# A gated state scan behind an attention layer: its plan of steps rearranged, with two gate buffers and the transposed product kept in its source's tile

## The chip, the cores and the metric

The kernel runs on one core of one Trainium2 chip. The metric is the device time in microseconds (us) of one execution. The chip's engines run side by side, each through its own queue in order: PE (TensorE: matrix products, PEld being its weight loads), DVE (VectorE), ACT (ScalarE), POOL (GpSimd) and SP, which only issues DMA transfers here. They wait for each other through semaphores.

## What is computed

Two layers are added to a residual stream `x` of 8 batches, 1024 time steps and 512 channels in float32. The first is a modulated attention; the change doesn't touch it. The second, cut to what matters:

```python
xr, gate = jnp.split(x @ W_in.T, 2, axis=-1)          # 1024 + 1024 channels
xc = jax.nn.silu(conv4(xr + t_emb) + b_conv)          # causal, 4 taps, by channel
xn = (xc - mu) / jnp.sqrt(var + 1e-05) * ln_g + ln_b
Bm, Cm, dt = jnp.split(xn @ W_xproj.T, 3, axis=-1)    # 16 states
dt = jnp.tanh(dt @ W_dt.T + b_dt) * 0.01
Ad = 1.0 + dt * A                                     # A = -tanh(A_log)
Bd = Bm * jnp.minimum(norm(xn), 1.0)
h = jnp.clip(h * ad[:, :, None] + bd[:, :, None] * xt[:, None, :], -10.0, 10.0)   # over time
yt = jnp.einsum('bd,bdh->bh', ct, h)
y = ys + D * xn
return y * jax.nn.silu(gate) @ W_out.T
```

The recurrence in `h` must run through the 1024 time steps one after the other. Its state is 8 batches x 16 states = 128 rows by 1024 channels, one tile of the chip's 128 partitions.

## The kernel before

`network` runs `modulated_attention` and then `gated_scan`. Inside `gated_scan` the order is written by hand: `at(n, f, ...)` (line 492) puts a piece of work into the list of step n, and the last loop (line 818) walks through the steps, issuing first `step(n)`, the recurrence, and then the pieces of step n in the order in which they were put there. Each engine's queue has exactly this order, so a piece that waits holds up all that comes after it on the same engine.

A chunk is 32 time steps (`TC`) of all 8 batches; there are 32 chunks. A chunk has two halves (i = 0 and 1) of 16 steps, each a tile of 128 rows (16 times x 8 batches). `n0` is the first step of a chunk and `p0 = n0 - 32`, so the pieces put at `p0 + ...` prepare a chunk while the one before runs, and those at `n0 + ...` or later finish it. Steps are counted within a chunk, 0 to 31, below. The pieces are:

- Preparation: `load_x1` (512 KB of the stream, by DMA), eight input products with the convolution (`conv_mm` on PE, `conv_in` on ACT, `conv_taps` on DVE, `conv_out` on ACT), then the normalization by halves: `flip_mm` (PE transposes, "x flips"), `stats` and `center` (DVE), `deviation`, `scale` (which also stores the tile `xt` as `xd` in HBM), `squares` (ACT), and `skip` (DVE, `xt` times D). `p_mm`, `p_out`, `p_flip`, `lengths`, `params`, `params_mm` and `params_out` make the 48 parameters of each time step; `spread` sends them over the partitions with eight small DMAs into `bca`; `decay` turns them into factors (tanh on ACT at line 630, then seven DVE instructions), and `weights` fills the weights `yw` of the state products.
- Recurrence: `fetch` brings four time steps at once, spread over the 16 states, with eight DMAs of 256 KB (three buffers `xb`); `weigh` scales one step's row on ACT two steps ahead; `step` is one DVE instruction that writes `h` (line 755; a pool `hp` of six buffers); `products`, the state products on PE, read four `h` tiles at once at steps 0, 4, 8, ... and add up `y_ps`.
- Output by halves: `order` (ACT) copies the stream in the half's row order into `x1t`; `gate_mm` (PE, two halves of 512 columns) and `gate` (ACT, silu) make the gate; `gate_y` (DVE) adds `y_ps` to `xt` and multiplies by the gate; `out_flip` (PE) and `out_copy` (ACT) transpose the product into `gT`; `out_mm` (PE, two halves, the first with an identity product that adds the stream) makes `o_ps`; `out_store` copies and stores it.

The tiles in question: `gate` and `gT` have one buffer each, `xt` four, `x1t` two, `y_ps` two (two PSUM banks each), and all other PE outputs share the four remaining banks (tag "mm"). Every DMA is issued by SP, in the plan's order.

The plan around the change is in lines 762 to 811; the gate's and the output's pieces are placed by two lines:

```python
g0 = n0 + (4, 20)[i]          # order at g0, gate products at g0 + 3 and g0 + 5
e0 = n0 + TT * i + TT         # gate_y at e0 + 2, flips at e0 + 4, 5, output products at e0 + 7, 9
```

Of the kernel before, what the change touches and what calls it, by code (L numbers as in the profile page):

```python
# [8 lines left out]
F32 = mybir.dt.float32  # L9
# [6 lines left out]
P = 128  # L16
# [5 lines left out]
DI = 1024  # L22
KI = DI // P
NS = 16
TC = 32
TT = 16
# [338 lines left out]
def gated_scan(ctx, tc, const, x1_d, S, w_in, w_conv, cols, ln_g, ln_b, w_x, w_xd, w_dt, b_dt, a_log,  # L365
# [10 lines left out]
    nc = tc.nc  # L376
    NCH = S // TC
    CW = B * TC
    NT = TC // TT
# [3 lines left out]
    one = ctx.enter_context(tc.tile_pool(name="s1", bufs=1))  # L383
    two = ctx.enter_context(tc.tile_pool(name="s2", bufs=2))
    hp = ctx.enter_context(tc.tile_pool(name="hp", bufs=6))
    xcp = ctx.enter_context(tc.tile_pool(name="xcp", bufs=2))
    xtp = ctx.enter_context(tc.tile_pool(name="xtp", bufs=4))
# [30 lines left out]
    na = load(a_log, "na", [P, 1])  # L418
    wx_sb = wp.tile([P, KI, NX], F32, name="wx")
    nc.sync.dma_start(out=wx_sb[:, :, 0 : 2 * NS], in_=w_x.rearrange("(k p) o -> p k o", p=P))  # L420
    wxd = one.tile([NS, DI], F32, tag="gT", name="wxd")
    nc.sync.dma_start(out=wxd, in_=w_xd)
    wdt = load(w_dt, "wdt", [NS, NS])
    my_sb = load(mask_y, "mask_y", [P, B])
# [67 lines left out]
    def at(n, f, *args):  # L492
        plan.setdefault(n, []).append(lambda: f(*args))
# [173 lines left out]

    def gate(st, i, half):
        if half == 0:
            st["gate", i] = one.tile([P, DI], F32, name="gate")  # L670
        nc.scalar.activation(
            st["gate", i][:, half * 512 : (half + 1) * 512], st.pop(("g", i, half)), AF.Silu
        )

    def gate_y(st, i):
        xt, g = st.pop(("xt", i)), st["gate", i]
        nc.vector.tensor_add(xt, st.pop(("y", i)), xt)
        nc.vector.tensor_mul(g, xt, g)  # L678

    def out_flip(st, i, half):  # L680
        ps = st["gt", i, half] = ps_m.tile([P, 4, P], F32, tag="mm", name="gt_ps")
# [3 lines left out]

    def out_copy(st, i, half):
        if half == 0:
            st["gT", i] = one.tile([P, KI, P], F32, tag="gT", name="gT")
        nc.scalar.copy(st["gT", i][:, 4 * half : 4 * half + 4, :], st.pop(("gt", i, half)))  # L689

    def out_mm(st, i, half):
# [70 lines left out]
    for c in range(NCH):  # L762
        st, n0 = sts[c], c * TC
        p0 = n0 - TC
        if c > 0:
            at(p0 - 11, load_x1, st, c)
        at(p0 - 9, begin, st)
        for k in range(KI):
            at(p0 - 8 + 2 * k, conv_mm, st, k)
            at(p0 - 7 + 2 * k, conv_in, st, k)  # L770
            at(p0 - 5 + 2 * k, conv_taps, st, k)
            at(p0 - 4 + 2 * k, conv_out, st, k)
        for i in range(NT):
            f0 = p0 + 11 + 3 * i
            at(f0, flip_mm, st, i, 0)
            at(f0, flip_mm, st, i, 1)
            at(f0 + 1, stats, st, i, 0)
            at(f0 + 1, stats, st, i, 1)
            at(f0 + 1, center, st, i)
            at(f0 + 2, deviation, st, i)  # L780
            at(f0 + 3, scale, st, i)
            at(f0 + 4, squares, st, i)
            at(f0 + 7 + i, skip, st, i)
        at(p0 + 12, p_mm, st)
        at(p0 + 13, p_out, st)
        at(p0 + 15, p_flip, st)
        at(p0 + 19, lengths, st)
        for i in range(NT):
            at(p0 + 20 + i, params, st, i)
            at(p0 + 21 + i, params_mm, st, i)  # L790
            at(p0 + 22 + i, params_out, st, i)
        at(p0 + 23, spread, st)
        at(p0 + 26, decay, st)
        at(p0 + 28, weights, st, 0)
        at(n0 + 4, weights, st, 1)
        for i in range(NT):
            g0 = n0 + (4, 20)[i]
            at(g0, order, st, i)
            for half in range(2):
                at(g0 + 3 + 2 * half, gate_mm, st, i, half)  # L800
                at(g0 + 5 + 2 * half, gate, st, i, half)
            e0 = n0 + TT * i + TT
            at(e0 + 2, gate_y, st, i)
            for half in range(2):
                at(e0 + 4 + half, out_flip, st, i, half)
                at(e0 + 5 + half, out_copy, st, i, half)
                at(e0 + 7 + 2 * half, out_mm, st, i, half)
            at(e0 + 11, out_store, st, c, i)
    for g in range(S // 4):
        at(4 * g - 9, fetch, g)  # L810
        at(4 * g + 4, products, g)
# [13 lines left out]
@with_exitstack  # L825
def network(ctx: ExitStack, tc: tile.TileContext, S, ins, out):
    nc = tc.nc
    const = ctx.enter_context(tc.tile_pool(name="const", bufs=1))
    dram = ctx.enter_context(tc.tile_pool(name="dram", bufs=1, space=DRAM))
    x1_d = dram.tile([S // TC, H, B, TC], F32, name="x1_d")  # L830
    xu_d = dram.tile([2, H, S], F32, name="xu_d")
    ident = const.tile([P, P], F32, name="ident")
    nc.sync.dma_start(out=ident, in_=ins["ident"])
    sT = const.tile([P, 2 * KH, B], F32, name="sT")
    nc.sync.dma_start(out=sT, in_=ins["condT"].rearrange("(k p) b -> p k b", p=P))
    with tc.manual_schedule():
        modulated_attention(
            tc, const, x1_d, xu_d, S, ins["xT"], {n: ins[f"w{n}T"] for n in "qkvwu"}, ident, sT
        )
        gated_scan(  # L840
            tc, const, x1_d, S, ins["w_in"], ins["w_conv"],
            {n: ins[f"{n}_c"] for n in ("b_conv", "ln_g", "ln_b")}, ins["ln_g"], ins["ln_b"],
            ins["w_x"], ins["w_xd"], ins["w_dt"], ins["b_dt"], ins["a_log"], ins["d_skip"],
            ins["w_out"], ident, ins["cond"], ins["pick"], ins["mask_y"], out,
        )
# [62 lines left out]
```

## Time and profile before

| | |
|---|---|
| median of 3 runs | 6852.26 us (6847.03 to 6880.9) |
| the profiled execution | 6840.93 us, span 6838.9 us |
| mean granted TensorE clock | 0.947 |
| PE, DVE, ACT busy in 5000 to 6000 us | 849, 761, 648 us |
| DMA engines busy there, and what they moved | 0.78, 202 GB/s |
| the recurrence instruction (line 755) | 1024 x 1342 ns, 587.5 us idle before it |
| the scaling (line 731) | 1024 x 1140 ns |
| gate products (line 663), output products (line 701) | 460.5 and 468.0 us in all |

A span is the time from the first to the last instruction. A chunk of the second layer takes some 95 us, and the second layer some 3100 of the 6839 us. "Busy" is the time in which an engine executes; "idle before" a group of instructions is what its engine stood still just ahead of them, with the instruction that released it. In the timeline a row gives the start in us from the start of the span, the length, the engine, the line, the operation, the tiles (written <- read) and, in brackets, the idle time and the releaser.

### The profile page before, as it was taken

The numbers are of one execution on the slowest core, as the hardware profiler recorded it, in microseconds if no ns is written. First come the engines' busy times: TensorE is split into PE (matmuls) and PEld (weight loads), VectorE is DVE, ScalarE is ACT, GpSimd is POOL, SyncE is SP. The second block draws the span as 40 slices with busy tenths as digits, with TensorE's granted clock in tenths as the row PEclk, the third lists the DMA queues.
The fourth block names the chain that finished last, engine by engine and source line by source line (L and its number), as shares of the span: only waits on it lengthen the run. The fifth ranks groups of instructions, "written<-read, shape, count | busy, mean of one in ns | idle before, by whom it ended". The sixth has DMA issues, their size and how long they took to land.

```text
span 6838.9 us, 113125 instructions
## 1 busy us (share of the span) xinstructions
PE 6072.8 (89%) x42960; PEld 3291.8 (48%) x42960; DVE 4499.3 (66%) x6851; ACT 3919.7 (57%) x6713; POOL 1333.6 (20%) x1220
## 2 busy tenths in 40 slices
PE   7889989899899898998997788888888888888887
PEld 4555545555555455555554444444434444444443
DVE  2656656656566566565664677777777777777776
ACT  3555545545555455555553566666666666666665
POOL 2343333423433334234332000000000000000000
PEclk9999999999999999999999898999889998899898
DMA  2011111111111111111112777778777787777776
GB/s 67 18 32 50 46 43 41 30 55 44 33 49 46 43 44 29 57 43 37 44 34 75 192 202 202 199 197 208 202 196 204 199 209 200 196 203 196 202 205 174
DMA packets 493518, 777.47 MB, mean 114 GB/s; under 512 B 197008, under 2 KB 295448, under 8 KB 492976
## 3 DMA queue, kind: packets, MB, share of 16 engines
q1 hardware_dynamic: 492976, 770.22, 43.3%
q8 instruction: 342, 5.60, 0.3%
q14 instruction: 200, 1.64, 0.1%
HBM read 659.40 MB, written 83.89 MB: 109 GB/s over the span
## 4 chain that ended last, share of the span: by engine, by line
PE 64%; DVE 17%; DMA 7%; ACT 4%; issue 4%; SPq 2%; POOL 1%; DVEq 0%; ACTq 0%; POOLq 0%
PE mm_ps L107 17%; PE t_ps L245 12%; PE s_ps L235 7%; PE av L252 7%; DVE h L755 7%; PE o_ps L701 5%; PE g_ps L663 4%; DMA xb<-xd 4%; PE y_ps L742 3%; PE in_ps L508 3%; DVE nmax L327 2%; PE p_ps L539 2%; SPq L724 1%; ACT xb L731 1%; DVE gate L678 1%
## 5 line engine op out<-in xcount | busy, mean ns | idle before, releaser
L755 DVE CUSTOM_DVE_ANT_0 h<-h,xb,lim 128x1024 f32<-128x1024 f32 x1024 | 1374.1, 1342 | 587.5 <-ACT xb L731 335.2
L327 DVE TENSOR_REDUCE nmax<-s_ps 128x1 f32<-128x1024 f32 x1024 | 1205.0, 1218 | 767.6 <-PE s_ps L238 763.7
L356 POOL TENSOR_SCALAR pr<-pr,rinv 128x1024 f32<-128x1024 f32 x1024 | 1148.2, 1122 | 2279.5 <-PE t_ps L245 1515.8
L245 PEld LDWEIGHTS t_ps<-ident,pr 128*128 128x128 f32 x8192 | 904.7, 141 | 868.1 <-issue 609.0
L245 PE MATMUL t_ps<-ident,pr 128*128 128x128 f32 x8192 | 1156.7, 280 | 170.3 <-DVE pT L338 124.8
L336 ACT ACTIVATE pr<-s_ps,nmax 128x1024 f32<-128x1024 f32 x1024 | 1141.5, 1115 | 83.9 <-DVE nmax L327 60.3
L731 ACT ACTIVATE xb<-xb,ws 128x1024 f32<-128x1024 f32 x1024 | 1154.0, 1140 | 30.8 <-DMA xb<-xd 30.8
L333 ACT COPY pT<-t_ps 128x512 f32<-128x512 f32 x512 | 300.1, 586 | 1313.6 <-PE t_ps L245 1313.6
L742 PE MATMUL y_ps<-h,yw 128*32 128x512 f32 x4096 | 647.1, 720 | 8.0 <-DVE h L755 8.0
L346 DVE COPY pT<-t_ps 128x512 f32<-128x512 f32 x512 | 353.2, 690 | 399.9 <-PE t_ps L245 397.7
L235 PE MATMUL s_ps<-kT,qT 32*128 32x512 f32 x2048 | 579.7, 640 | 0.0
L238 PE MATMUL s_ps<-k,q 32*128 32x512 f32 x2048 | 577.1, 640 | 0.0
L252 PE MATMUL av<-pT,vt 128*32 128x128 f32 x16384 | 559.2, 278 | 0.4 <-DVE aT L319 0.4
L508 PE MATMUL in_ps<-x,win 128*128 128x256 f32 x2048 | 543.2, 412 | 3.6 <-DMA x<-x_d 2.8
L508 PEld LDWEIGHTS in_ps<-x,win 128*128 128x128 f32 x2048 | 401.2, 205 | 162.8 <-issue 59.2
L701 PE MATMUL o_ps<-wout,gT 128*128 128x512 f32 x1024 | 468.0, 600 | 0.5 <-ACT gT L689 0.5
L252 PEld LDWEIGHTS av<-pT,vt 128*32 128x32 f32 x16384 | 420.1, 110 | 88.0 <-issue 86.6
L663 PE MATMUL g_ps<-win,x1t 128*128 128x512 f32 x1024 | 460.5, 592 | 0.4 <-ACT x1t L658 0.4
L527 DVE SCALAR_TENSOR_TENSOR xc<-xr,cw,xc 128x256 f32<-128x256 f32 x768 | 370.7, 483 | 26.7 <-ACT xc L520 8.4
L338 DVE COPY pT<-t_ps 128x512 f32<-128x512 f32 x512 | 348.4, 680 | 2.6 <-PE t_ps L245 2.6
L347 ACT COPY pT<-t_ps 128x512 f32<-128x512 f32 x512 | 297.4, 581 | 82.2 <-PE t_ps L245 82.2
L684 PE MATMUL gt_ps<-ident,gate 128*128 128x128 f32 x512 | 108.8, 350 | 243.7 <-DVE gate L678 243.7
(128 smaller groups left out, 6381.5 us busy)
## 6 DMA issues: line engine op xcount, KB each, us to landing
xb<-xd SPq DMA_DIRECT2D x2048, 256.0 KB
xd<-xt SPq DMA_DIRECT2D x64, 512.0 KB
xh<-in_xT SPq DMA_DIRECT2D x16, 1024.0 KB
q<-qT SPq DMA_DIRECT2D x128, 128.0 KB
xr<-in_xT SPq DMA_DIRECT2D x64, 256.0 KB
xu_d<-xr SPq DMA_DIRECT2D x64, 256.0 KB
xr<-xu_d SPq DMA_DIRECT2D x64, 256.0 KB
x_d<-xr SPq DMA_DIRECT2D x64, 256.0 KB
```

What stands on the lines that cost most here:

```text
L107: nc.tensor.matmul(ps, w, x, start=(k == 0), stop=(k == KH - 1))
L235: nc.tensor.matmul(s_ps[i][:, 0:HW], st["q"][r, qc], st["k"][r, 0:HW], start=True, stop=True)
L245: nc.tensor.transpose(ps[:, j], pr[:, c0 : c0 + P], ident)
L252: nc.tensor.matmul(av[r], vt[:, kt, r], pT[:, i, kt], start=(kt == 0), stop=(kt == KT - 1), skip_group_check=True,)
L327: nc.vector.tensor_reduce(nmax[i], s_ps[i], AX.X, ALU.max, negate=True)
L336: nc.scalar.activation(fresh[i], s_ps[i], AF.Exp, bias=nmax[i], accum_out=rsum[i])
L356: nc.gpsimd.tensor_scalar(fresh[i], fresh[i], rinv[i], 1.0, ALU.mult, ALU.mult)
L508: nc.tensor.matmul(ps, win_sb[:, kk, k * P : (k + 1) * P], st["x1"][:, kk].rearrange("p b t -> p (b t)"), start=(kk == 0), stop=False,)
L701: nc.tensor.matmul(ps, st["gT", i][:, k, :], wout_sb[:, k, :], start=False, stop=(k == KI - 1), skip_group_check=True,)
L731: nc.scalar.mul(xbs[n], xbs[n], sts[c]["ws"][:, t : t + 1])
L742: nc.tensor.matmul(st["y", i][32 * r : 32 * r + 32, hf * 512 : (hf + 1) * 512], yws[i][:, 4 * q + r, :], hs[4 * g + r][:, hf * 512 : (hf + ...
L755: nc.vector._custom_dve(dve_ops.TENSOR_ADD_SAT, out=h, in0=last["h"], in1=xbs.pop(n), s0=lim[:, 0, t : t + 1], s1=lim[:, 1, t : t + 1],)
```

## The change

The pieces of the plan are moved, and some tiles change. The first gate product of half 0 goes from step 7 to 1 and the second from 9 to 5; those of half 1 from 23 and 25 to 22 and 23. `gate_y` is split into `add_y` and `gate_y`, a step or two apart; half 0 is at 23 and 24 (before 18), half 1 at 8 and 10 of the next chunk (before 2). The output products of half 0 go from 23 and 25 to 27 and 29, those of half 1 from 7 and 9 to 13 and 15. The `gate` tile gets two buffers, since it now lives longer; the transposed product has no tile `gT` of its own any more and is written into the tile `xt` of its half, and `wxd`, which shared that buffer at the start, moves to the pool of `xt`. In the preparation the second half's normalization stands four steps after the first one's (before three), `skip` at 19 and 25 (before 18 and 22), and the parameters' pieces from `p_mm` to `weights` one step later, `spread` among them. On PE the number of products is the same.

```diff
--- before.py
+++ after.py
@@ -418,7 +418,7 @@
     na = load(a_log, "na", [P, 1])
     wx_sb = wp.tile([P, KI, NX], F32, name="wx")
     nc.sync.dma_start(out=wx_sb[:, :, 0 : 2 * NS], in_=w_x.rearrange("(k p) o -> p k o", p=P))
-    wxd = one.tile([NS, DI], F32, tag="gT", name="wxd")
+    wxd = xtp.tile([NS, DI], F32, tag="xt", name="wxd")
     nc.sync.dma_start(out=wxd, in_=w_xd)
     wdt = load(w_dt, "wdt", [NS, NS])
     my_sb = load(mask_y, "mask_y", [P, B])
@@ -667,15 +667,17 @@
 
     def gate(st, i, half):
         if half == 0:
-            st["gate", i] = one.tile([P, DI], F32, name="gate")
+            st["gate", i] = two.tile([P, DI], F32, name="gate")
         nc.scalar.activation(
             st["gate", i][:, half * 512 : (half + 1) * 512], st.pop(("g", i, half)), AF.Silu
         )
 
+    def add_y(st, i):
+        nc.vector.tensor_add(st["xt", i], st.pop(("y", i)), st["xt", i])
+
     def gate_y(st, i):
-        xt, g = st.pop(("xt", i)), st["gate", i]
-        nc.vector.tensor_add(xt, st.pop(("y", i)), xt)
-        nc.vector.tensor_mul(g, xt, g)
+        g = st["gate", i]
+        nc.vector.tensor_mul(g, st["xt", i], g)
 
     def out_flip(st, i, half):
         ps = st["gt", i, half] = ps_m.tile([P, 4, P], F32, tag="mm", name="gt_ps")
@@ -685,7 +687,7 @@
 
     def out_copy(st, i, half):
         if half == 0:
-            st["gT", i] = one.tile([P, KI, P], F32, tag="gT", name="gT")
+            st["gT", i] = st.pop(("xt", i)).rearrange("p (k t) -> p k t", k=KI)
         nc.scalar.copy(st["gT", i][:, 4 * half : 4 * half + 4, :], st.pop(("gt", i, half)))
 
     def out_mm(st, i, half):
@@ -771,7 +773,7 @@
             at(p0 - 5 + 2 * k, conv_taps, st, k)
             at(p0 - 4 + 2 * k, conv_out, st, k)
         for i in range(NT):
-            f0 = p0 + 11 + 3 * i
+            f0 = p0 + 11 + 4 * i
             at(f0, flip_mm, st, i, 0)
             at(f0, flip_mm, st, i, 1)
             at(f0 + 1, stats, st, i, 0)
@@ -780,32 +782,33 @@
             at(f0 + 2, deviation, st, i)
             at(f0 + 3, scale, st, i)
             at(f0 + 4, squares, st, i)
-            at(f0 + 7 + i, skip, st, i)
-        at(p0 + 12, p_mm, st)
-        at(p0 + 13, p_out, st)
-        at(p0 + 15, p_flip, st)
-        at(p0 + 19, lengths, st)
+            at(p0 + (19, 25)[i], skip, st, i)
+        at(p0 + 13, p_mm, st)
+        at(p0 + 14, p_out, st)
+        at(p0 + 16, p_flip, st)
+        at(p0 + 20, lengths, st)
         for i in range(NT):
-            at(p0 + 20 + i, params, st, i)
-            at(p0 + 21 + i, params_mm, st, i)
-            at(p0 + 22 + i, params_out, st, i)
-        at(p0 + 23, spread, st)
-        at(p0 + 26, decay, st)
-        at(p0 + 28, weights, st, 0)
+            at(p0 + 21 + i, params, st, i)
+            at(p0 + 22 + i, params_mm, st, i)
+            at(p0 + 23 + i, params_out, st, i)
+        at(p0 + 24, spread, st)
+        at(p0 + 27, decay, st)
+        at(p0 + 29, weights, st, 0)
         at(n0 + 4, weights, st, 1)
-        for i in range(NT):
-            g0 = n0 + (4, 20)[i]
-            at(g0, order, st, i)
+
+        for i, (xo, gm, gs, ey) in enumerate(
+            ((-2, (1, 5), (3, 7), (23, 24, 25, 27)), (17, (22, 23), (24, 25), (40, 42, 43, 45)))
+        ):
+            at(n0 + xo, order, st, i)
+            at(n0 + ey[0], add_y, st, i)
+            at(n0 + ey[1], gate_y, st, i)
             for half in range(2):
-                at(g0 + 3 + 2 * half, gate_mm, st, i, half)
-                at(g0 + 5 + 2 * half, gate, st, i, half)
-            e0 = n0 + TT * i + TT
-            at(e0 + 2, gate_y, st, i)
-            for half in range(2):
-                at(e0 + 4 + half, out_flip, st, i, half)
-                at(e0 + 5 + half, out_copy, st, i, half)
-                at(e0 + 7 + 2 * half, out_mm, st, i, half)
-            at(e0 + 11, out_store, st, c, i)
+                at(n0 + gm[half], gate_mm, st, i, half)
+                at(n0 + gs[half], gate, st, i, half)
+                at(n0 + ey[2] + half, out_flip, st, i, half)
+                at(n0 + ey[2] + 1 + half, out_copy, st, i, half)
+                at(n0 + ey[3] + 2 * half, out_mm, st, i, half)
+            at(n0 + ey[3] + 4, out_store, st, c, i)
     for g in range(S // 4):
         at(4 * g - 9, fetch, g)
         at(4 * g + 4, products, g)
```

## The prediction

> **What bounds the kernel now.** I read the page first. The work splits near 3750 us, where POOL falls silent and the DMA share rises from 1 to 7 tenths. The diff touches only the second part.
>
> ```profile
> PE 6072.8 (89%) x42960; PEld 3291.8 (48%) x42960; DVE 4499.3 (66%) x6851; ACT 3919.7 (57%) x6713; POOL 1333.6 (20%) x1220
> ...
> POOL 2343333423433334234332000000000000000000
> ...
> DMA  2011111111111111111112777778777787777776
> ...
> PE 64%; DVE 17%; DMA 7%; ACT 4%; issue 4%; SPq 2%; POOL 1%; DVEq 0%; ACTq 0%; POOLq 0%
> ```
>
> No engine is saturated in that part. By the windows view, 5000 to 6000 us has PE busy 849 us, VectorE 761, ScalarE 648, DMA engines 0.78. So the limit must alternate. The next view is the timeline of VectorE over one chunk (start us, length, engine, line, tiles, then idle time and releaser). The lines are the recurrence steps h(2), h(6), h(10), ... of a chunk; I number them from h(18), the only one followed by the add, the gate product and a skip product (L677, L678, L595; 5199.96).
>
> ```profile
> 5152.00 1.34 DVE L755 CUSTOM_DVE_ANT_0 h<-h,xb,lim 128x1024 f32<-128x1024 f32 x1
> ...
> 5163.35 1.34 DVE L755 CUSTOM_DVE_ANT_0 h<-h,xb,lim 128x1024 f32<-128x1024 f32 x1 [0.53 <-PE y_ps L742]
> ...
> 5176.10 1.34 DVE L755 CUSTOM_DVE_ANT_0 h<-h,xb,lim 128x1024 f32<-128x1024 f32 x1 [4.15 <-ACT xs L534]
> ...
> 5189.38 1.35 DVE L755 CUSTOM_DVE_ANT_0 h<-h,xb,lim 128x1024 f32<-128x1024 f32 x1 [1.35 <-PE y_ps L742]
> ...
> 5199.96 1.34 DVE L755 CUSTOM_DVE_ANT_0 h<-h,xb,lim 128x1024 f32<-128x1024 f32 x1
> ...
> 5210.68 1.34 DVE L755 CUSTOM_DVE_ANT_0 h<-h,xb,lim 128x1024 f32<-128x1024 f32 x1
> ...
> 5224.01 1.34 DVE L755 CUSTOM_DVE_ANT_0 h<-h,xb,lim 128x1024 f32<-128x1024 f32 x1 [6.52 <-ACT xb L731]
> ...
> 5237.96 1.34 DVE L755 CUSTOM_DVE_ANT_0 h<-h,xb,lim 128x1024 f32<-128x1024 f32 x1
> ...
> 5246.48 1.34 DVE L755 CUSTOM_DVE_ANT_0 h<-h,xb,lim 128x1024 f32<-128x1024 f32 x1
> ```
>
> The reader should take differences: 11.35, 12.75, 13.28, 10.58, 10.72, 13.33, 13.95 and (5237.96 to 5246.48) 8.52 us; in all 94.48 us a chunk. Brackets hold the waits: 0.53, 4.15, 1.35, 6.52. Step h(n) overwrites the h buffer of step n-6 (six buffers), which the state product of its group reads (L742, planned at steps 0, 4, 8, ...). So at every h(4g+2) VectorE waits until PE has finished everything queued ahead of product 4g. The chunk is eight such meetings, and each stretch lasts as long as the slower of the two engines.
>
> The PE timeline of the same chunk shows how much that is, and the other cost:
>
> ```profile
> 5155.88 1.09 PE L684 MATMUL gt_ps<-ident,gate 128*128 128x128 f32 x4 [3.14 <-DVE gate L678]
> 5156.76 3.62 PE L508 MATMUL in_ps<-x,win 128*128 128x256 f32 x8
> ...
> 5163.65 1.89 PE L508 MATMUL in_ps<-x,win 128*128 128x256 f32 x8
> ...
> 5170.53 3.60 PE L663 MATMUL g_ps<-win,x1t 128*128 128x512 f32 x8
> ...
> 5219.46 1.97 PE L508 MATMUL in_ps<-x,win 128*128 128x256 f32 x8 [0.29 <-DMA x<-x_d]
> ...
> 5223.83 3.70 PE L701 MATMUL o_ps<-wout,gT 128*128 128x512 f32 x8
> ```
>
> A warm input product is 2.5 us (5163.65, with its 0.69 us end piece), a gate product 3.43 to 3.6, a second output product 3.54 to 3.7. After the idle 3.14 us before 5155.88 the same input product takes 3.62 instead of 1.89. The granted clock of 5155.8 to 5161 is 0.50, of 5161 to 5180 it is 1.00.
>
> Last the SP queue of the same chunk:
>
> ```profile
> 5206.11 5.01 SPq L724 DMA_DIRECT2D xb<-xd  x8
> 5211.23 0.57 SPq L401 DMA_DIRECT2D x<-x_d  x1
> 5214.37 5.53 SPq L626 DMA_DIRECT2D bca<-few  x8
> 5220.01 5.49 SPq L724 DMA_DIRECT2D xb<-xd  x8
> ```
>
> The x1 load goes out behind eight fetches (5.0 us after h(19)); the chain of waits gives its transfer 8.09 us, to 5219.34, and PE takes it up at 5219.46 after idling 0.29.
>
> **What the Trainium skill says.** (1) "TensorE: Matmul & The Clock Gate", "HAM oscillation": PE idle for more than about 3.4 us falls back to half clock. The trace agrees: 3.14 us idle was followed by clock 0.50 and doubled durations. (2) Same page, "Architectural detail": ScalarE and VectorE are strict FIFO. Agrees: the scaling of xb stood at 5222.87 behind a gate activation and a conversion that waited 1.29 and 2.34 us for PE. (3) "DMA: Bandwidth & Descriptors", "Queues, rings and completion order": each DMA engine takes descriptors in ring order, so a small load waits behind large ones. Agrees: 8.09 us for x1's 512 KB, behind 2 MB of fetches.
>
> **The change, by stretch.** No arithmetic is removed or added: the sum, product, flips and copies are the same, only split or renamed. I price units from start to next start in those timelines. VectorE: h 1.26 (1.51 if another h follows), taps 1.43, add 1.20, gate product 1.14 (2.39 together), skip 1.14, statistics and centring 2.90, small rs 0.27, scale 1.19, nr 0.60, parameters 0.82, decay 1.49, yw 0.41. PE: input product 2.50, state product 1.85, gate product 3.43, output product 4.43 (first half, with its identity part) and 3.54, gate flip 0.50, x flips 0.97, p 3.58, pt 0.34, xp 0.49. Each stretch (us) runs from h(4g-2) to h(4g+2); PE's load is what it must do after one state product up to and with the next.
>
> | to | VectorE before | PE before | measured | VectorE after | PE after |
> |---|---|---|---|---|---|
> | h(2) | 8.40 | 6.85 | 8.52 | 8.40 | 10.39 |
> | h(6) | 10.70 | 7.35 | 11.35 | 8.56 | 10.28 |
> | h(10) | 8.40 | 12.71 | 12.75 | 9.35 | 7.78 |
> | h(14) | 8.71 | 13.37 | 13.28 | 9.60 | 3.82 |
> | h(18) | 10.59 | 3.16 | 10.58 | 9.65 | 14.71 |
> | h(22) | 10.81 | 2.35 | 10.72 | 8.79 | 1.85 |
> | h(26) | 6.93 | 13.69 | 13.33 | 9.34 | 12.19 |
> | h(30) | 9.80 | 13.82 | 13.95 | 10.30 | 12.28 |
>
> Example: to h(26) before, PE has flip 0.50, xp 2 x 0.49, output 4.43, gate 3.43, input 2.50, state 1.85 = 13.69. After, the output half and the flip are gone from it and the second gate half has come in: 2 x 3.43 + 0.98 + 2.50 + 1.85 = 12.19. The larger of the two, summed: before 94.09 (measured 94.48), after 10.39 + 10.28 + 9.35 + 9.60 + 14.71 + 8.79 + 12.19 + 12.28 = 87.59. That is 6.5 us a chunk less, because the four stretches where gate and output halves stood together (12.7 to 13.8) are spread over five, and one of them (to h(18)) becomes the worst at 14.71.
>
> What gives some of it back, with bounds:
> - To h(18): first output half, p and second output half stand ahead of the second x flips. The statistics of step 16 wait for those flips and are followed by 2.90 us of VectorE, so the stall comes late in the stretch. Output half 1 may start when state product 12 is done, about 1.9 us after h(12). Then flips end 4.43 + 3.58 + 3.54 + 0.97 = 12.5 later, 14.4; with 2.90 and h(17) 1.53, h(18) is 18.8 after h(12). The table has h(12) to h(18) at 5.69 (4.16 + 1.53) + 14.71 = 20.4, so nothing is lost: 0. Against that, gate flips (step 11) wait for the product of step 10: PE is done 7.78 after h(6), that product ends at 9.35 + 1.26 + 1.14 = 11.75, so PE idles 4.0, longer than the 3.14 that preceded clock 0.50. Flips, state product 12 and the start of the output half then run slow: 0 to 3 us, I take 1.2.
> - To h(26): less PE work ahead uncovers the x1 load. h(19) ends 3.7 after h(18); + 5.0 issue + 8.1 transfer + 2.50 + 1.85 = 21.2, against 8.79 + 12.19 = 20.98. I take 0.3; if the load's wait (some 3 us of idle PE) cools the clock, up to 2.5 more. Nothing the change does moves that load; its old release, the reordering copy one step before it, now stands four steps before and never was last.
> - ScalarE, FIFO: h(n+1) of an odd step waits for a scaling queued behind the conversion that needs PE's input product; where PE leads the stretch (to h(2), h(6)) that is 0 to 1, I take 0.3.
> - The spread of bca is one step later, so on SP it is behind the fetch of step 23 (5.0 us), not ahead of it. Behind its tanh on ScalarE stand a conversion and the scaling of h(29); behind decay on VectorE stand taps and h(28). x1 lands at 3.7 + 5.0 + 8.1 = 16.8 after h(18); the last fetch and then the last spread follow. With 6.51 us for a fetch (chain of waits) the last spread is issued near 24, and lands at most 4.0 later (before, 5219.90 to the tanh at 5223.91 without a wait). Tanh near 26.5 (25 to 28), then 0.3 + decay 1.49 + taps 1.43 + h 1.51 + h, yw, taps 3.10 = 7.8: h(30) at 34.3 against 20.98 + 12.28 = 33.3. Some of that overlaps the x1 term; I take 0.5, bounds 0 and 3.
> - Second gate buffer, transposed product in xt (its gate product has been read before the copy, by order), wxd: cost 0, hidden since the tiles' previous users are ten steps or more back; the one tight one, centring at step 16 into xt whose last reader is the output half of step 15, follows x flips that stand behind that half on PE anyway. At the start and end of the part: once, a few us either way, 0.
>
> Sum: -6.5 + 1.2 + 0.3 + 0.3 + 0.5 = -4.2 us a chunk. Of 32 chunks 31 are whole periods: -130 us. Against the profiled execution (span 6838.9, time 6840.93) that is 6711; the median of the runs is 11.3 above it, so 6852 - 130 = 6722.
>
> **Rivals.**
> A, forecast: 6722, its own range 6680 to 6770 (terms at -5.5 to -2.7).
> B, the give-back is hidden: the bare -6.5 x 31 = -200, 6650. For it: before, the bare sum missed by only 0.4 although that chunk had three cooled PE stretches (clock 0.50, 0.66 and 0.67 in 5155.8 to 5161, 5195 to 5200 and 5203 to 5212). Against: before, those cooled stretches fell where VectorE led, and the x1 load was just covered.
> C, the cold clock and x1 take most: terms of 4.5 up to 3 + 2.8 + 0.5 = 6.3, so -2 to 0 a chunk, 6790 to 6852. For it: idle 3.14 us sufficed to halve the clock. Against: PE's queue after the idle is mostly what has 5 us to spare (9.60 against 3.82).
> D, slower: bca. If the eight pieces, queued behind 2 MB, land one after another and not within 4.0, tanh comes past 30 instead of 26.5. The gain to h(30) is 38.0 measured (5199.96 to 5237.96) minus 33.3; the other five stretches give only 56.48 - 54.33 = 2.2, less 1.5 of the terms. So no gain is left from h(30) at 38.0 + 0.7 (tanh at 30.9); with tanh at 33 it is +2.1 us a chunk, +65, about 6917. For it: SP and DMA share 0.9 in 5222 to 5250. Against: pieces of 6 KB landed in 4.0 or less behind x1.
>
> **How the numbers follow.** A 0.50, B 0.17, C 0.19, D 0.14. Time: that of A, 6722. The range leaves out the better part of D's and a corner of B's: 6630 (B, 20 lower) to 6870 (C and D's beginning). A measurement here can tell about 0.5%, 34 us. Faster: A, B and half of C, 0.77; the rest of C 0.09; D 0.14.
>
> **What would show it.** Right: stretches near the last columns; output and gate halves no longer adjacent on PE; a stretch to h(18) of 14 to 16 us with the statistics (L557) waiting for x flips; PE waiting for the x1 DMA some 3 us a chunk; chunk period 89 to 91. Wrong: a wait of ScalarE at L630 for bca over 4 us (D); granted clock low from step 11 to 14 and the stretch over 18 us (C); a period under 88 (B).

## The result and the profile after

The changed kernel takes 6810.5 us (median of 6 runs, 6805.32 to 6819.54) against 6846.35 before (6842.43 to 6880.9, 6 runs): a ratio of 0.9931 (0.9911 to 0.9952), 36 us or 0.7% faster. The forecast was 130 us faster. So the direction is right, the size is less than a third of it, and the time lies where rival C put it (6790 to 6852).

The page of the profiled execution (span 6817.7 us); for the groups the columns are count, busy time, mean ns, idle time before and its releaser:

```profile
PE 6117.6 (90%) x42960; PEld 3331.8 (49%) x42960; DVE 4491.4 (66%) x6851; ACT 3915.2 (57%) x6713; POOL 1329.4 (19%) x1220
...
PEclk9999999999999999999999799999999999999999
DMA  2011111111111111111112787878878778888787
...
L757 DVE CUSTOM_DVE_ANT_0 h<-h,xb,lim 128x1024 f32<-128x1024 f32 x1024 | 1374.2, 1342 | 582.5 <-ACT xb L733 305.0
...
L508 PE MATMUL in_ps<-x,win 128*128 128x256 f32 x2048 | 548.2, 415 | 116.7 <-DMA x<-x_d 116.7
```

The clock line has got better (nearly all 9; before, several slices of the second part were 8), but the input product (L508) now stands 116.7 us behind the DMA of x1, where before 2.8 of its 3.6 idle us were put to that. Next the timeline of VectorE for one chunk, the same eight meetings h(2), h(6), ..., h(30), h(2) as before the change:

```profile
5152.01 1.34 DVE L757 CUSTOM_DVE_ANT_0 h<-h,xb,lim 128x1024 f32<-128x1024 f32 x1
...
5162.39 1.34 DVE L757 CUSTOM_DVE_ANT_0 h<-h,xb,lim 128x1024 f32<-128x1024 f32 x1
...
5172.78 1.34 DVE L757 CUSTOM_DVE_ANT_0 h<-h,xb,lim 128x1024 f32<-128x1024 f32 x1
...
5182.41 1.34 DVE L757 CUSTOM_DVE_ANT_0 h<-h,xb,lim 128x1024 f32<-128x1024 f32 x1
...
5198.57 1.34 DVE L757 CUSTOM_DVE_ANT_0 h<-h,xb,lim 128x1024 f32<-128x1024 f32 x1
...
5207.06 1.34 DVE L757 CUSTOM_DVE_ANT_0 h<-h,xb,lim 128x1024 f32<-128x1024 f32 x1
...
5221.76 1.34 DVE L757 CUSTOM_DVE_ANT_0 h<-h,xb,lim 128x1024 f32<-128x1024 f32 x1 [5.44 <-ACT xb L733]
...
5233.97 1.34 DVE L757 CUSTOM_DVE_ANT_0 h<-h,xb,lim 128x1024 f32<-128x1024 f32 x1
...
5244.38 1.34 DVE L757 CUSTOM_DVE_ANT_0 h<-h,xb,lim 128x1024 f32<-128x1024 f32 x1
```

The differences are 10.38, 10.39, 9.63, 16.16, 8.49, 14.70, 12.21 and 10.41 us. The bracket at h(26) is to be read with care: the scaling of that step had ended 7.8 us earlier (the one that ends at 5221.76 is that of step 27), and what ended 0.11 us before h(26), in this chunk and in the mean of 28, is PE's state product of step 24.

The table puts the means over 28 chunks (third to thirtieth), worked out from the starts of the recurrence instruction in the timelines, beside the larger of the two loads of the prediction:

| stretch to | before | forecast load | after | after minus load |
|---|---|---|---|---|
| h(6) | 11.90 | 10.28 | 10.38 | 0.10 |
| h(10) | 12.46 | 9.35 | 10.38 | 1.03 |
| h(14) | 13.28 | 9.60 | 9.63 | 0.03 |
| h(18) | 10.58 | 14.71 | 15.91 | 1.20 |
| h(22) | 10.74 | 8.79 | 8.49 | -0.30 |
| h(26) | 13.00 | 12.19 | 16.17 | 3.98 |
| h(30) | 13.95 | 12.28 | 12.45 | 0.17 |
| h(2) | 8.54 | 10.39 | 10.36 | -0.03 |
| chunk | 94.45 | 87.59 | 93.77 | 6.18 |

Five stretches are within 0.3 us of their loads. One has nearly all of the loss: h(22) to h(26), where the first input product of the next chunk needs x1. SP's queue and PE's timeline in that place (the rows before 5200 belong to the stretches before it and are used further down):

```profile
5202.39 5.04 SPq L726 DMA_DIRECT2D xb<-xd  x8
5207.54 0.52 SPq L401 DMA_DIRECT2D x<-x_d  x1
5210.42 5.78 SPq L726 DMA_DIRECT2D xb<-xd  x8
5216.78 8.06 SPq L626 DMA_DIRECT2D bca<-few  x8
```

```profile
5175.40 1.09 PE L686 MATMUL gt_ps<-ident,gate 128*128 128x128 f32 x4 [5.41 <-DVE gate L680]
5176.28 1.91 PE L552 MATMUL x_ps<-ident,xs 128*128 128x128 f32 x8
...
5193.51 1.04 PE L552 MATMUL x_ps<-ident,xs 128*128 128x128 f32 x8
...
5215.79 3.38 PE L508 MATMUL in_ps<-x,win 128*128 128x256 f32 x8 [3.74 <-DMA x<-x_d]
5219.10 0.69 PE L512 MATMUL in_ps<-few 8*128 8x256 f32 x2
```

Between h(18) and h(22) nothing is new: eight fetches go out behind h(19), then x1. But PE is now through with its gate products and the last parameter flip some 3.7 us before x1 is there, and the input product then runs in 3.38 us instead of 1.89. It was slow like this (over 2.5 us) in 27 of the 28 chunks. In 15 of them the state product behind it was slow too; PE's timeline of such a stretch, of 17.8 us:

```profile
5868.39 3.75 PE L508 MATMUL in_ps<-x,win 128*128 128x256 f32 x8 [4.24 <-DMA x<-x_d]
...
5873.22 3.64 PE L744 MATMUL y_ps<-h,yw 128*32 128x512 f32 x16
```

Here the state product takes 3.64 us, where it takes 1.92 at the full clock. The windows view (us, busy us of PE, its loads, VectorE, ScalarE, POOL; then granted clock, DMA share, GB/s) shows both sides:

```profile
5495.30:5498.20 2.90, 0.15 (x2) 0.01 (x1) 2.90 (x3) 2.50 (x6) 0.00 (x0) 1.00 1.08 316
5498.20:5502.30 4.10, 4.08 (x10) 2.73 (x10) 1.51 (x2) 0.00 (x0) 0.00 (x0) 0.58 1.05 272
5868.40:5876.80 8.40, 8.40 (x27) 3.60 (x27) 0.01 (x1) 1.88 (x3) 0.00 (x0) 0.50 0.92 202
```

While PE stands still (first row) the DMA engines move 316 GB/s, at a share of 1.08: x1's 512 KB come behind the 2 MB of fetches. After an idle stretch of only 2.8 us the clock over the next 4.1 us is 0.58, and after 4.24 us it is 0.50 for 8.4 us. The waits view of 4000 to 6500 us (total, times, longest) gives the sizes:

```profile
PE gt_ps L686 <- DVE gate L680: 146.1, 27, 5.4
...
PE in_ps L508 <- DMA x<-x_d: 100.3, 26, 5.8
...
ACT bca L630 <- DMA bca<-few: 22.2, 14, 4.2
```

The second largest loss is in the stretch to h(18). Rows of ScalarE and VectorE in it, from the timeline of the same chunk:

```profile
5190.08 0.36 ACT L542 COPY few<-p_ps 48x256 f32<-48x256 f32 x1 [7.76 <-PE p_ps L539]
5190.38 1.15 ACT L733 ACTIVATE xb<-xb,ws 128x1024 f32<-128x1024 f32 x1
...
5191.56 1.34 DVE L757 CUSTOM_DVE_ANT_0 h<-h,xb,lim 128x1024 f32<-128x1024 f32 x1 [5.36 <-ACT xb L733]
5194.15 1.30 DVE L557 BATCH_NORM_STATS2 stat<-x_ps 128x6 f32<-128x512 f32 x2 [1.24 <-PE x_ps L552]
```

PE's parameter product reaches VectorE by way of ScalarE: its copy (L542) waits 7.76 us in ScalarE's queue, the scaling of step 16 stands behind it, and h(16) waits 5.36 us for that scaling. After h(16) the statistics still wait 1.24 us for the x flips (32.0 us in 26 chunks by the waits view), so the flips are what came last.

### The profile page after: what moved, and what is told of

The parts are those of the page before. It is cut to its first block, busy times and chain, and to the rows that moved or that the text cites. A ratio compares the mean times of both kernels' runs of the same rounds, so it can differ in the third digit from the quotient of the medians.

```text
span 6817.7 us, 113117 instructions
## 1 busy us (share of the span) xinstructions
PE 6117.6 (90%) x42960; PEld 3331.8 (49%) x42960; DVE 4491.4 (66%) x6851; ACT 3915.2 (57%) x6713; POOL 1329.4 (19%) x1220
## 5 line engine op out<-in xcount | busy, mean ns | idle before, releaser
L508 PE MATMUL in_ps<-x,win 128*128 128x256 f32 x2048 | 548.2, 415 | 116.7 <-DMA x<-x_d 116.7
L508 PEld LDWEIGHTS in_ps<-x,win 128*128 128x128 f32 x2048 | 412.3, 207 | 259.6 <-issue 175.4
L703 PE MATMUL o_ps<-wout,xt 128*128 128x512 f32 x1024 | 469.3, 602 | 0.0
L744 PEld LDWEIGHTS y_ps<-h,yw 128*32 128x32 f32 x4096 | 130.5, 117 | 466.7 <-issue 252.6
```

Source lines behind the costliest of these rows:

```text
L508: nc.tensor.matmul(ps, win_sb[:, kk, k * P : (k + 1) * P], st["x1"][:, kk].rearrange("p b t -> p (b t)"), start=(kk == 0), stop=False,)
L744: nc.tensor.matmul(st["y", i][32 * r : 32 * r + 32, hf * 512 : (hf + 1) * 512], yws[i][:, 4 * q + r, :], hs[4 * g + r][:, hf * 512 : (hf + ...
```

## The experiments

All times are medians; the ratios are to the kernel before, run on the same chip between them. The means of the stretches over the same 28 chunks are collected in a table at the end of this section.

**x1 load ahead of the fetch.** The change itself made room for this: the copy `order`, the last reader of the old x1 tile, moved from step 20 to 17.

```diff
-            at(p0 - 11, load_x1, st, c)
+            at(p0 - 13, load_x1, st, c)
```

> The changed kernel with the x1 load put at step 19 ahead of that step's fetch instead of step 21 behind it. Theory X (the late x1 load is what took the gain: 115 us of idle PE over 30 chunks, and a cooled clock after it): PE no longer waits for the DMA of x1, the stretch h(22) to h(26) falls from 16.2 us on average to the 12.2 to 13 of the table, and the kernel becomes 3.3 to 4 us a chunk faster than the change, about 6690 us. Rival Y (the spread and its tanh stand right behind and take over): the stretch to h(26) falls but that to h(30) grows by as much, the sum changes by under 1.5 us a chunk, over 6765 us. Rival Z (the cold clock comes from elsewhere): the DMA wait goes, the input product stays at 3.4 us, some 6730 us.

6599.58 us, ratio 0.9617 (0.959 to 0.9643): 7.1 us a chunk less than the change, more than any theory had. SP's queue and PE's timeline of a chunk:

```profile
5182.04 0.33 SPq L582 DMA_DIRECT2D xd<-xt  x1
5182.48 0.38 SPq L401 DMA_DIRECT2D x<-x_d  x1
5183.30 13.09 SPq L726 DMA_DIRECT2D xb<-xd  x16
```

```profile
5192.79 1.89 PE L508 MATMUL in_ps<-x,win 128*128 128x256 f32 x8
5194.61 0.69 PE L512 MATMUL in_ps<-few 8*128 8x256 f32 x2
5195.23 1.92 PE L744 MATMUL y_ps<-h,yw 128*32 128x512 f32 x16
```

x1 goes out right behind the store of the second half. PE comes to the input product without a wait, at 1.89 us, and h(26) is reached in 9.31 us, about VectorE's own load of 9.34: since PE isn't held up, it starts the stretch ahead and its 12.19 us are no bound any more. Theory X holds for the cause, but it had 3.3 to 4 us a chunk and 12.2 us for the stretch. Rival Y was half right: the spread does come to stand next,

```profile
5206.38 0.24 DVE L631 TENSOR_SCALAR bca<-bca,na 128x32 f32<-128x32 f32 x1 [6.26 <-ACT bca L630]
```

and the stretch to h(30) grows from 12.45 to 17.10. But the following ones, to h(2), h(6) and h(10), shrink by 1.93, 1.67 and 0.76, because PE worked on during that wait.

**x1 load one step earlier, still behind the fetch.**

```diff
-            at(p0 - 11, load_x1, st, c)
+            at(p0 - 12, load_x1, st, c)
```

> The changed kernel with the x1 load one step earlier in the plan (20 instead of 21), but still behind the fetch of step 19 in SP's queue. Theory X in its strict form (the fetch in front of it sets the load's time, not the plan's step): nothing changes, within 0.3% of the change, 6810 us, and the PE wait for x1 stays at 3.8 us a chunk. Rival: the step matters, each step earlier gives some 2 us a chunk, 6750 us.

6804.92 us, 0.9916 (0.9886 to 0.9946): no difference to the change that the times can tell, and PE still waits 91.9 us for x1 in 26 chunks (before this edit 100.3). In the profile a chunk is 0.9 us shorter (92.87 us), most of it in the stretch to h(26) (15.42). It is the fetch in front of the load that sets its time, far more than the plan's step.

**The spread ahead of the fetch.**

```diff
-        at(4 * g - 9, fetch, g)
+        at(4 * g - 9 + (g % 8 == 0), fetch, g)
```

> The changed kernel with the fetch of step 23 moved to step 24, so that the spread's eight small DMAs stand ahead of it as before the change. Theory: the spread behind the fetch costs little inside the chunks (the wait of line 630 for bca was 22 us in 26 chunks), but 8 us once, since the first recurrence step came at 3843.8 instead of 3835.4; so 10 to 30 us faster than the change, 6780 to 6800 us, with the first step back at about 3835. Rival (bca is what the chunk pays): over 60 us faster. Rival (the fetch is needed in time): the recurrence waits for xb at steps 0 to 3 and it is slower, over 6830 us.

6757.38 us, 0.9843 (0.9809 to 0.9878), 53 us below the change and so between the theory and its rival. The waits view (total, times, longest):

```profile
PE in_ps L508 <- DMA x<-x_d: 80.1, 25, 4.0
...
DVE bca L631 <- ACT bca L630: 1.0, 2, 0.5
```

The wait for bca is gone (1.0 us), but it hadn't been worth 53 us. Most of the gain is in the stretch to h(26), 14.30 instead of 16.17. The two causes can be told apart in the timelines: the input product starts 16.61 us after h(18) instead of 17.32 (0.7 us), and from its start to the end of the state product PE needs 6.06 us instead of 7.24 (1.2 us), as it ran slow in 22 chunks of 28 instead of 27. Why x1 comes sooner was not tested; there is no fetch close behind it any more. The once-only cost isn't the point either: the time from the layer's first load to the first recurrence step was 83.9 us before, 90.1 after and 84.2 here.

**The parameter product later.**

```diff
-        at(p0 + 13, p_mm, st)
-        at(p0 + 14, p_out, st)
-        at(p0 + 16, p_flip, st)
+        at(p0 + 17, p_mm, st)
+        at(p0 + 18, p_out, st)
+        at(p0 + 19, p_flip, st)
```

> The changed kernel with the parameter product moved from step 13 to 17 (its copy to 18, its flip to 19), out of the stretch h(14) to h(18), where PE has 14.7 us of work, into h(18) to h(22), where it has 1.85. Theory (stretches last as long as the busier engine): h(14) to h(18) falls from 15.9 to 11.5 to 12.3, h(18) to h(22) stays under 9.5; 3 to 4 us a chunk, some 6700 us. Rival (the x1 load, timed from h(19), or the parameters' chain eats it): the stretch to h(26) grows by as much, under 1 us a chunk, over 6780 us.

6695.13 us, 0.9762 (0.973 to 0.9793), as the theory had it. PE's timeline:

```profile
5220.26 7.03 PE L703 MATMUL o_ps<-wout,xt 128*128 128x512 f32 x16
5227.13 1.04 PE L552 MATMUL x_ps<-ident,xs 128*128 128x128 f32 x8
...
5229.95 3.65 PE L539 MATMUL p_ps<-xs,wx 128*48 128x256 f32 x16
```

The second half's x flips follow the output products, and the parameter product comes after the state product of step 16. The stretch to h(18) falls from 15.91 to 12.11, that to h(22) stays at 8.55: the model of the busier engine holds for this stretch too.

**PE kept busy while it waits.** In `conv_mm`, for the first of the eight products only; the added products' results are overwritten:

```diff
         ps = st["in", k] = ps_m.tile([P, CW], F32, tag="mm", name="in_ps")
+        if k == 0:
+            for _ in range(7):
+                nc.tensor.matmul(ps, win_sb[:, 0, 0:P], win_sb[:, 1, 0:CW], start=True, stop=True, skip_group_check=True)
```

> The changed kernel with seven extra 128x256 products ahead of the first input product of a chunk, into its own bank before it starts (about 3.1 us of added PE work, its result overwritten), which need no x1 and so run while PE waits for x1. Theory (a part of the price of the late load is the clock that falls during the wait): the first input product takes 1.9 instead of 3.4 to 3.75 us, the stretch h(22) to h(26) falls by 1 to 2.5 us, 40 to 70 us faster than the change, about 6755 us, though work was added. Rival (only the arrival of x1 counts): the product is no faster or the stretch no shorter; the added work costs 0 to 1 us a chunk, 6810 to 6840 us.

6701.61 us, 0.9768 (0.9749 to 0.9787): 109 us faster than the change with more work in it, twice the expected. PE's timeline:

```profile
5158.13 3.19 PE L509 MATMUL in_ps<-win 128*128 128x256 f32 x14
5161.36 1.99 PE L511 MATMUL in_ps<-x,win 128*128 128x256 f32 x8
5163.28 0.69 PE L515 MATMUL in_ps<-few 8*128 8x256 f32 x2
5163.91 1.92 PE L747 MATMUL y_ps<-h,yw 128*32 128x512 f32 x16
```

The seven added products (L509; each of them is two instructions in this view) fill the gap. x1 comes nearly as late as ever: the real product starts 16.82 us after h(18), against 17.32. But it takes 1.99 us and its state product 1.92, and it was slow in none of the 28 chunks. So of the 7.1 us a chunk that the early load brings, 3.9 (93.77 to 89.87) come without an earlier load. In the stretch to h(26) the gain is 3.27 us: 2.8 are the products that no longer run at half clock, and 0.5 are the somewhat earlier x1, whose cause is open.

**Both DMA moves.** Edits one and three together.

> The changed kernel with the x1 load at step 19 and the spread ahead of the fetch of step 23. With the x1 load alone PE runs unbroken from step 22 to 8, while VectorE waits 6.6 us a chunk for bca. Theory P (PE's run hides most of that wait): only the time between the end of state product 8 and the end of the gate product of step 10 can go, 3.5 us a chunk at most: 83 us a chunk, 6490 us. Rival (the wait for bca is on the path with its whole length): 80 us a chunk, 6400 us. Rival (all hidden): 6590 us.

6589.85 us, 0.9602 (0.9585 to 0.9619), against 0.9617 with the x1 load alone: no gain that the times can tell, the last rival. PE's unbroken run from step 22 to 8 had hidden the 6.3 us wait for bca all but 0.5 us a chunk (86.70 to 86.17). The bound that I gave (3.5) took it that an earlier h(10) would help. It comes no earlier: h(9) waits 0.9 us a chunk for its scaling, which stands on ScalarE behind the conversion of the last input product of that run. The state product of step 8 ended 2.8 us before h(10).

**All three moves.** Edits one, three and four.

> The changed kernel with all three moves: x1 load at step 19 ahead of the fetch, the spread ahead of the fetch of step 23, the parameter product at step 17. Theory (gains add up until PE's unbroken run from step 22 to 8, 52.7 us, and the way round it bind): about 3.3 us a chunk below the kernel with the first two moves, 80 us a chunk, some 6390 us, faster than both kernels. Rival (VectorE's 74 us and the DMA engines' 74 us a chunk bind first): over 83 us a chunk, over 6480 us.

6489.91 us, 0.9448 (0.9421 to 0.9475). 81.9 us a chunk, 1.9 more than expected, since the base of that sum, the kernel with both DMA moves, is at 86.2 and not at 83. Against that base the parameter product gives 4.25 us. The time is on the rival's side of its line (6480 us), the chunk is not (83 us), so the two limits that it named are not shown to bind. In the waits view PE still has

```profile
PE gt_ps L686 <- DVE gate L680: 157.0, 29, 5.5
```

5.4 us a chunk before the gate flip.

**The preparation as before the change.** The changed kernel with the preparation's steps of the kernel before; output, buffers and tiles as changed:

```diff
-            f0 = p0 + 11 + 4 * i
+            f0 = p0 + 11 + 3 * i
...
-            at(p0 + (19, 25)[i], skip, st, i)
+            at(f0 + 7 + i, skip, st, i)
...
-        at(p0 + 24, spread, st)
-        at(p0 + 27, decay, st)
+        at(p0 + 23, spread, st)
+        at(p0 + 26, decay, st)
```

> The changed kernel with the preparation's pieces put back where they were before (second half three steps after the first, skip at 18 and 22, parameters, spread and decay one step earlier), the output's pieces, buffers and tiles as changed. Theory: the shift by one step, which put the spread behind the fetch of step 23, is a part of what the change lost; undone, the once-only 8 us and the wait of line 630 go, and the x1 load has no fetch close behind it: like the kernel with the spread first, 6740 to 6780 us. Rival (the shift is needed for the second x flips, which would now stand ahead of the output half): the stretch h(14) to h(18) changes by over 1.5 us either way, outside 6740 to 6780.

6762.08 us, 0.9845 (0.9817 to 0.9872), as expected and like the kernel with the spread first. The shift of the preparation, taken whole, cost about 50 us. The rival's sign appeared too, without its time: the stretch to h(18) fell by 1.56 us (14.35 instead of 15.91), but that to h(14) grew by 2.59 (12.22 instead of 9.63). The gain is in the stretch to h(26), at 13.39: PE stands idle 2.16 us before the input product instead of 3.85, and the product was slow in 5 chunks of 28 instead of 27.

**The second half's gate and output earlier.** On top of the three moves:

```diff
-((-2, (1, 5), (3, 7), (23, 24, 25, 27)), (17, (22, 23), (24, 25), (40, 42, 43, 45)))
+((-2, (1, 5), (3, 7), (23, 24, 25, 27)), (17, (22, 23), (24, 25), (37, 39, 41, 43)))
```

> The kernel with all three moves, and of the second half's output the add at step 5, the gate product at 7, flips at 9 and 10, output products at 11 and 13 (before: 8, 10, 11 and 12, 13 and 15). In the kernel with all three moves PE still stands 5.4 us a chunk before the gate flip, waiting for the gate product of step 10. Theory: the wait falls by 3 us or more and its work is put into the stretch h(10) to h(14); by the larger of the two engines that stretch becomes 11.8 and h(14) to h(18) 9.65, so a gain of 0 to 1 us a chunk, 6455 to 6490 us. Rival (the idle of PE is lost time with its whole length): 3 us a chunk and more, under 6400 us. Rival (the extra VectorE work in h(2) to h(10) delays PE's products there): slower, over 6500 us.

And the same with that half's second output product at 47 and its store at 49:

> As the kernel before, with the second output product at step 15 instead of 13, so that h(10) to h(14) has 8.25 us of PE work and h(14) to h(18) 6.7, both under VectorE's 9.6. Theory: 1.4 us a chunk less than with all three moves, 80.5 us a chunk, some 6440 us. Rival (VectorE's work of h(2) to h(10) and the x flips, which wait for the last input product's activation, bind): no gain, 6480 to 6500 us.

6433.64 us, 0.9385 (0.9361 to 0.941), and 6432.87, 0.9385 (0.9363 to 0.9408): 80.06 us a chunk both. The first gained more than expected (1.86 us a chunk, between its theory and its first rival): PE was ahead again, so the stretch to h(14) took 8.76 and not 11.8, while that to h(6) grew by 1.13 with the add in it. The placing of the second output product makes no difference: with the slack of both stretches it is hidden either way. They are the fastest kernels here, 6% under the one before. The windows view of 4000 to 6000 us, first the changed kernel and then the first of these two:

```profile
4000.00:6000.00 2000.00, 1747.68 (x7374) 866.71 (x7373) 1528.52 (x2163) 1308.04 (x2227) 0.00 (x0) 0.93 0.81 202
```

```profile
4000.00:6000.00 2000.00, 1908.93 (x8597) 933.38 (x8596) 1790.44 (x2523) 1534.20 (x2599) 0.00 (x0) 1.00 0.93 237
```

The clock is at 1.00, the DMA engines at 0.93 and VectorE at 1790 of 2000 us.

In the table the last three rows follow the first input product of a chunk in the same 28 chunks: its start after h(18), the time from there to the end of the state product, and the number of chunks in which it took over 2.5 us. They show the arrival of x1 and the clock apart.

| stretch to | after | x1 early | spread first | p later | kept warm | both DMA | all three | gate earlier |
|---|---|---|---|---|---|---|---|---|
| h(6) | 10.38 | 8.71 | 10.38 | 10.39 | 10.31 | 10.38 | 10.39 | 11.51 |
| h(10) | 10.38 | 9.62 | 10.39 | 10.39 | 10.38 | 10.39 | 10.39 | 9.69 |
| h(14) | 9.63 | 9.63 | 9.64 | 9.64 | 9.63 | 9.64 | 9.64 | 8.76 |
| h(18) | 15.91 | 15.42 | 15.84 | 12.11 | 15.44 | 15.36 | 11.11 | 9.70 |
| h(22) | 8.49 | 8.49 | 8.49 | 8.55 | 8.49 | 8.49 | 8.55 | 8.55 |
| h(26) | 16.17 | 9.31 | 14.30 | 16.01 | 12.90 | 9.32 | 9.25 | 9.25 |
| h(30) | 12.45 | 17.10 | 12.15 | 12.41 | 13.70 | 12.10 | 12.13 | 12.12 |
| h(2) | 10.36 | 8.43 | 10.51 | 10.34 | 9.02 | 10.51 | 10.48 | 10.49 |
| chunk | 93.77 | 86.70 | 91.68 | 89.82 | 89.87 | 86.17 | 81.92 | 80.06 |
| start after h(18) | 17.32 | 13.31 | 16.61 | 17.51 | 16.82 | 13.31 | 13.31 | 13.31 |
| start to end | 7.24 | 4.37 | 6.06 | 6.94 | 4.46 | 4.37 | 4.37 | 4.37 |
| slow, of 28 | 27 | 0 | 22 | 27 | 0 | 0 | 0 | 0 |

## Why the prediction was right and wrong

- The model (a stretch lasts as long as the busier of PE and VectorE between two meetings) held in its numbers: five of eight stretches within 0.3 us, and the stretch to h(18) at 15.91, inside the 14 to 16 us that were named. The longest in the mean is that to h(26), 16.17. The experiments bear the model out where the load was changed (p later: 12.11). It is too high where PE can start ahead (x1 early: 9.31 against 12.19).
- The way in which the engines meet is only in part the one that was given. After the change VectorE's long wait for the state product itself is that at h(26) (6.9 us a chunk). Its other long waits are before h(1), h(5), h(9) and h(16): 2.10, 1.60, 0.89 and 5.12 us. They end 0.03 us (median) after that step's scaling on ScalarE, which stands behind a conversion or copy that waited for PE. PE's load still sets the time, but ScalarE's queue hands it on.
- The step that failed is the term "To h(26)": "I take 0.3; if the load's wait (some 3 us of idle PE) cools the clock, up to 2.5 more". The wait and its place were right, the size was not: the sum put the cold clock at nothing. The term measured 3.98, above the 2.8 of its bound (3.68 together with the stretch to h(22) before it). The arrival of x1 was nearly right: PE takes it up 17.32 us after h(18), against 16.8. What was mis-sized is what follows it. From there to the end of the state product the prediction has 2.50 + 1.85 = 4.35 us, and it took 7.24, since the wait cooled the clock in 27 of 28 chunks and it stayed low for 8.4 us in the window shown. With PE kept busy it took 4.46. The Trainium skill's page "TensorE: Matmul & The Clock Gate" (section on HAM oscillation) names an idle time of about 3.4 us. Here waits of 2.8 us, and of 3.14 before the change, were enough, while one of 3.44 us did not cool the clock, so the length of the wait alone does not decide it; the last section has the numbers. The sentence "Nothing the change does moves that load" was also incomplete: the change put a fetch 2.9 us behind it (5210.42 against 5207.54), and with the spread in its place the stretch is 14.30.
- To h(18), "I take 1.2": 1.20. PE did idle before the gate flip, 5.41 us rather than 4.0, and the x flips behind it took 1.91 instead of 1.04. That the term fits to the digit is luck; its bounds were 0 and 3. The parameter product's copy on ScalarE, which stops h(16), was not foreseen, but the x flips came later still.
- ScalarE, "I take 0.3": 1.03 to h(10), where VectorE has the larger load and h(9) waits 0.90 us for a scaling behind the last conversion. To h(2) and h(6), where it was expected, such waits are there (2.10 and 1.60 us), but they add next to nothing to PE's load (-0.03 and 0.10).
- bca, "I take 0.5": 0.17 in the stretch to h(30), about 0.9 us a chunk of wait at L630. Rival D never came near. But the reason given against it was not tested; what the runs show is that such a wait is hidden behind PE's run even at 6.3 us, all but 0.5 us a chunk.
- The sum: -6.5 (table) + 6.18 (measured terms), against the 2.3 taken. The middle chunks went from 94.45 to 93.77, or 21 us for 31 of them; the spans of the two profiles differ by 21.2 us as well. The other 15 us of the 36 are not seen in the profiles and may be the spread of the runs. The first layer, which no kernel here touches, ended between 3751.6 and 3785.8 us in these profiles, so single profiles differ by up to 34 us for that alone.
- The prediction said that the trace agrees with the 3.4 us of the page, beside an idle time of 3.14 us. The clock did fall there, but 3.14 is less than 3.4, so it was a sign that the figure is no safe limit.
- Rival C was the case that came about, by the mechanism it named, the cold clock and x1; its sign, a low clock from step 11 to 14 with a stretch over 18 us, came only in part, as that stretch took 15.91 us and the cold clock cost most at x1. It deserved more than 0.19, as the profile before had shown both that 3.14 us cools the clock and that x1 was only just in time (0.29 us).

SP's issue time and the bytes ahead of the load can be told apart in the packet records of the traces. With the load ahead of the fetch, it is issued 3.0 us after h(18) instead of 9.1, and its last packet ends 4.3 us after the issue instead of 7.2. So the place in SP's queue was worth 6.1 us of x1's earlier arrival and the bytes ahead of it 2.9.

## What to carry to other kernels

Where engines meet every few steps, add up each engine's load between the meetings. The sum of the larger ones gave the loop's time before the change to half a percent (94.09 against 94.45), and tells where to move work; after the change it was 6.2 us too low (87.59 against 93.77), because a late transfer and the clock are no part of it. When a stretch is relieved, look for the transfer that the old load just covered and move its issue together with the work: here two steps of plan, ahead of one fetch, were worth six times the whole change. A wait of the matrix engine costs its length and then the cold clock behind it, which here was 2.8 us for a wait of 3.9.

## What the runs showed of the hardware

The clock was 1.00 or 0.50 in the clock records of the second layer, and it changed only at the bounds of slices of 3.413 us that follow one another without a break. Two waits of PE for x1 in the changed kernel, cut at these bounds:

```profile
5495.14:5498.56 3.42, 0.65 (x5) 0.36 (x4) 3.42 (x4) 2.66 (x6) 0.00 (x0) 1.00 1.08 306
5498.56:5501.97 3.41, 3.41 (x9) 2.32 (x8) 1.15 (x2) 0.00 (x0) 0.00 (x0) 0.50 1.02 261
5583.88:5587.30 3.42, 1.77 (x7) 0.65 (x5) 3.42 (x4) 3.39 (x7) 0.00 (x0) 1.00 1.02 251
5587.30:5590.71 3.41, 1.62 (x8) 1.44 (x8) 2.62 (x3) 0.71 (x2) 0.00 (x0) 1.00 1.09 280
5590.71:5594.12 3.41, 3.41 (x26) 1.36 (x25) 0.47 (x1) 1.87 (x3) 0.00 (x0) 1.00 1.03 241
```

The first wait, of 2.77 us, lay in one slice, PE was busy for 0.65 us of it, and the next slice ran at 0.50. The second, of 3.44 us, was split over two slices with 1.77 and 1.62 us of work, and the clock stayed at 1.00. All twelve traces fit this, from 3900 us to near their ends, with PE's share of each slice worked out from the starts and ends of its instructions. Of the slices at 1.00, those with PE busy for less than 0.40 of their length (468) were all followed by 0.50, those with more than 0.60 (7852) never, and of the 442 between them 21 were. So in these runs it was PE's share of the slice that counted, and a wait of given length could go either way. How long the clock then stays low is not explained: slices at 0.50 with PE busy for less than 0.75 (298) were all followed by another, but so were 65 of the 433 with PE busy for 0.95 or more.

Seven useless products (3.2 us) in the gap made the kernel 109 us faster. A 512 KB load behind 2 MB of fetches was taken up by PE 8.25 us after its issue (5207.54 to 5215.79), while the DMA engines' share was 1.06.
